# A GNN layer whose gathers are shared out: SyncE copies one more pair of tiles per 16 octets, row by row

## The chip, the core and the metric

The kernel runs on one core of a Trainium2 chip. The metric is the device time of one execution in microseconds (us); lower is better. TensorE, VectorE, ScalarE, GpSimd and SyncE appear in the profile as PE (PEld for its weight loads), DVE, ACT, POOL and SP.

## The reference

One layer of a graph network with 12500 nodes of 64 features and 400000 edges of 16 features; the edges are sorted by their target node dst, their source nodes src are random. Afterwards x gets the layer's result added and is normalised.

```python
m_in = jnp.concatenate([x[src], x[dst], edge_attr], axis=-1)
h = jax.nn.silu(m_in @ W1 + b1)
messages = jax.nn.silu(h @ W2 + b2)
agg = jax.ops.segment_sum(messages, dst, num_segments=x.shape[0])
node_in = jnp.concatenate([x, agg], axis=-1)
y = jax.nn.silu(node_in @ W3 + b3)
x = _layernorm(x + y, axis=-1)
```

W1 is 144 x 64: its first 64 rows (W1a below) act on x[src], the next 64 on x[dst], the last 16 on the edge's own features.

## The kernel before

The edges come in 3125 tiles of 128. Eight tiles make an octet (391 octets, the last with five tiles), three octets a chunk. Because dst is sorted, the targets of a chunk lie in a window of 112 nodes.

The product x W1a is made once, in the first octets, and stored in device memory as the table pa, 12500 rows of 64 floats (256 bytes). From octet 9 on (RAW) an octet needs, for each of its 1024 edges, the row of pa (or, equally, of x) that src names. There are two ways to get it.

- `gather` (L290 to L300): GpSimd issues one indirect DMA per tile, which fetches 128 rows by a column of indices into `ga`. The tile pool of `ga` has AHEAD + 2 = 5 buffers, and octet o + 3 is gathered in the loop's pass o, so a gather waits until TensorE has read the octet five before it.
- `columns` (L245 to L266): for the first two tiles of some octets (the list `pairs`, 153 octets), ScalarE and VectorE copy columns of x, which lies transposed in SBUF as `xs`, into a tile `cx`. Each copy moves 4 bytes in 64 partitions from an address in a register. ScalarE copies 2 x 24 columns per octet and VectorE 2 x 28. The registers are loaded many at a time (L261) from a row of byte offsets `cxi`, which SyncE fetches from src (`index`, L277) and VectorE scales (`address`, L285).

`first_layer` (L348) adds, on TensorE, the part of the window and of the edge's features (L357), the column pairs times W1a (L368) and the gathered rows, transposed by a product with the identity (L370, one product per two tiles). ScalarE applies silu (L374, tile `h`). `second_layer` (L377) multiplies by W2 (L383, L385), ScalarE applies silu again (L389, tile `m`), and `add_up` (L392) multiplies m by `eh`, which marks each edge's target within the window (L398). VectorE makes `oh` and `eh` by comparisons (`compare_dst`, L337; `compare_nodes`, L344).

`load` (L321) is SyncE's main work: for each octet it copies 448 KB of target indices into `dr` (L326, two buffers) and 64 KB of edge features into `oh` (L328, three buffers). Once per chunk it also loads the window's columns `xr` at an address from a register (`window_load`, L303 and L307).

Each engine executes its instructions in the order in which the loop over octets (L509) writes them; a `manual_schedule` keeps that order for TensorE, ScalarE, VectorE and SyncE. In pass o the order of the calls is: `index(o + 3)`, `gather(o + 3)`, `load(o + 2)`, `compare_dst(o + 1)`, VectorE's first columns, `first_layer(o)`, `compare_nodes(o + 1)`, VectorE's second columns, `add_up(o - 2)`, `second_layer(o - 1)`, `address(o + 2)`, and then work on the nodes that are complete (with loads `xa` and stores `out` on SyncE) at the passes given in a table `todo`.

Of the kernel before, what the change touches and what calls it, by code (L numbers as in the profile page):

```python
# [9 lines left out]
F32 = mybir.dt.float32  # L10
BF16 = mybir.dt.bfloat16
I32 = mybir.dt.int32
U8 = mybir.dt.uint8
AF = mybir.ActivationFunctionType
OP = mybir.AluOpType
# [3 lines left out]
ENG = mybir.EngineType  # L19

P = 128
# [6 lines left out]
RAW = 9  # L28
TABLES = 4
ACOLS = (24, 24)  # L30
VCOLS = (28, 28)
ALOAD = 16
XBASE = (0, 64 << 18)
XADDR = 35840
# [59 lines left out]
def windows(ctx, tc, ident, badi, pa, x, xt, src_c, src_row, dst_c, dst_row, attr_t, base, w1, b1, w2, b2, w3, b3, out, edges):  # L94
    nc = tc.nc
    N, D = x.shape
# [69 lines left out]
    def resident(s, c):  # L166
        w = min(XC, NP - c)
        nc.sync.dma_start(xs[s * D:(s + 1) * D, c:c + w], xt[:, c:c + w])
# [41 lines left out]
    for k in range(3):  # L210
        t = fast.tile([P, D], F32, name=f"xw{k}")
# [3 lines left out]
    octs = []  # L215
# [4 lines left out]
    with tc.tile_pool(name="gat", bufs=AHEAD + 2) as gat, tc.tile_pool(name="drp", bufs=2) as drp, \  # L220
# [4 lines left out]
            tc.tile_pool(name="ps2", bufs=2, space=PSUM) as ps2, \  # L225
            tc.tile_pool(name="psa", bufs=1, space=PSUM) as psa, \
            tc.tile_pool(name="cx", bufs=4) as cx, tc.tile_pool(name="cxi", bufs=3) as cxi, \
            tc.tile_pool(name="nx", bufs=2) as nx, tc.tile_pool(name="nv", bufs=1) as nv:
        got, loaded, made = {}, {}, {}


        RATE = sum(ACOLS) + sum(VCOLS)
        pairs = []
        while True:
            o = RAW + -(-2 * P * (len(pairs) + 1) // RATE) + 1
# [6 lines left out]
        def columns(o, eng, part):  # L242
# [5 lines left out]
            else:  # L248
                lo, n, copy = lo + sum(ACOLS) + sum(VCOLS[:part]), VCOLS[part], nc.vector.tensor_copy
            hi = lo + n  # L250
            while lo < hi:
                j, e0 = lo // (2 * P), lo % (2 * P)
                if j >= len(pairs):
                    return
                n = min(hi - lo, P - e0 % P, ALOAD if eng == ENG.Activation else P)
                if pairs[j] not in cols:
# [8 lines left out]
                    copy(t[h, 4 * e:4 * e + 4], xb[h, ds(r - (XBASE[s] + XADDR), 4)])  # L265
                lo += n  # L266

        def begun(o):

            first, behind = -(-(o - RAW) * RATE // (2 * P)), -(-(o + 1 - RAW) * RATE // (2 * P))  # L270
            return range(max(0, first), max(0, min(behind, len(pairs))))

        def index(o):
            for j in begun(o):
                t = cxi.tile([1, 2 * P], I32, name="cxi")
                e = octs[pairs[j]][1] * P
                nc.sync.dma_start(t, src_row[:, e:e + 2 * P])  # L277
                indices[j] = t

        def address(o):  # L280
            for j in begun(o):
                t = indices[j]
                for s in range(2):
                    h = slice(s * P, (s + 1) * P)
                    nc.vector.tensor_scalar(t[:, h], t[:, h], 4.0, float(XBASE[s] + XADDR), op0=OP.mult, op1=OP.add)  # L285
# [4 lines left out]
        def gather(o):  # L290
            c, t0, n, first, last = octs[o]
            ga = gat.tile([P, OT, D], F32, name="ga")
            sc = srcs[t0 // SCT][:, t0 % SCT:]
            if n % 2:
                nc.vector.memset(ga[:, n, :], 0.0)
            for i in range(2 if o in pairs else 0, n):
                nc.gpsimd.indirect_dma_start(  # L297
                    out=ga[:, i, :], out_offset=None, in_=x if o < RAW else pa[:, :],
                    in_offset=bass.IndirectOffsetOnAxis(ap=sc[:, i:i + 1], axis=0))
            got[o] = ga  # L300
# [32 lines left out]
        def compare_dst(o):  # L333
            c, t0, n, first, last = octs[o]
            n2 = n + n % 2
            dr, oh = loaded.pop(o)
            nc.vector.tensor_tensor(oh[0:W, :n2 * P], dr[:, :n2 * P], wn[0:W, c:c + 1].to_broadcast([W, n2 * P]),  # L337
                                    op=OP.is_equal)
            hots[o] = [oh]

        def compare_nodes(o):
            c, t0, n, first, last = octs[o]
            eh = ehp.tile([P, OT, W], F32, name="eh")
            nc.vector.tensor_tensor(eh[:, :n], winrow[c][:, None, :].to_broadcast([P, n, W]),  # L344
                                    dc[:, t0:t0 + n, None].to_broadcast([P, n, W]), op=OP.is_equal)
            hots[o].append(eh)

        def first_layer(o):  # L348
            c, t0, n, first, last = octs[o]
            n2 = n + n % 2  # L350
            k = n2 // 2
            ga = got.pop(o)
            oh, eh = hots.pop(o)
            p1 = ps1.tile([P, OT // 2, P], F32, name="p1")
            ohv = oh.rearrange("p (i s e) -> p s i e", s=2, e=P)
            for s in range(2):
                nc.tensor.matmul(p1[s * D:(s + 1) * D, :k], xw[c % 3], ohv[:, s, :k], start=True, stop=False,  # L357
                                 skip_group_check=True)
            if o < RAW:
                pt = mis.tile([P, OT // 2, P], F32, name="mm")  # L360
                for i in range(k):
                    nc.tensor.matmul(pt[:, i, :], ga[:, 2 * i:2 * i + 2, :].rearrange("p s d -> p (s d)"), ident,  # L362
                                     start=True, stop=True)
                xg = work.tile([P, OT // 2, P], F32, name="m")
                nc.vector.tensor_copy(xg[:, :k], pt[:, :k])
                nc.tensor.matmul(p1[:, :k], w1d, xg[:, :k], start=False, stop=True, skip_group_check=True)
            if o in pairs:
                nc.tensor.matmul(p1[:, 0, :], w1d, cols.pop(o), start=False, stop=False, skip_group_check=True)  # L368
            for i in range(1 if o in pairs else 0, k if o >= RAW else 0):
                nc.tensor.matmul(p1[:, i, :], ga[:, 2 * i:2 * i + 2, :].rearrange("p s d -> p (s d)"), ident,  # L370
                                 start=False, stop=(i == k - 1), skip_group_check=True)
            columns(o, ENG.Activation, 0)
            h = work.tile([P, OT // 2, P], F32, name="h")
            nc.scalar.activation(h[:, :k], p1[:, :k], AF.Silu, bias=b1s)  # L374
            made[o] = h, eh
# [106 lines left out]
        for q in range(early):  # L482
            o = lead[due[q]] + 2
# [4 lines left out]
        for q0 in range(0, rest, RB):  # L488
            o = lead[due[q0 + RB - 1]] + 2
# [16 lines left out]
        with tc.manual_schedule(engines={ENG.PE, ENG.Activation, ENG.DVE, ENG.SP}):  # L506
            compare_dst(0)
            compare_nodes(0)
            for o in range(NO + 1):  # L509
                if o == 0:  # L510
                    sources(0, slice(CT, SCT))
                    for c in range(0, NP, XC):
                        resident(0, c)
                    nc.sync.dma_start(dc[:, CT:], dst_c[:, CT:])
                    for k in range(0, NP, 2048):
                        n = min(2048, NP - k)
                        nc.scalar.activation(agg[:, k:k + n], zero.to_broadcast([P, n]), AF.Copy)
                for c in tables[o * per:(o + 1) * per]:
                    table(c)
                if o == RAW:  # L520
                    nc.vector.memset(mv, 1.0)
                    nc.vector.memset(eps, 1e-5)
                if 1 <= o < 1 + len(range(0, NP, XC)):
                    resident(1, (o - 1) * XC)
                index(o + 3)
                if o % (SCT // OT) == 6 and (o // (SCT // OT) + 1) * SCT < TILES:
                    sources(o // (SCT // OT) + 1)
                if o + AHEAD < NO:
                    gather(o + AHEAD)
                if o + 2 < NO:  # L530
                    load(o + 2)
                    if octs[o + 2][3]:
                        window_load(octs[o + 2][0])
                if o + 1 < NO:
                    compare_dst(o + 1)
                columns(o, ENG.DVE, 0)
                if o >= 3 and octs[o - 3][4]:
                    add_window(octs[o - 3][0])
                if o < NO:
                    first_layer(o)  # L540
                if o + 1 < NO:
                    if octs[o + 1][3] and o:
                        window_copy(octs[o + 1][0])
                    compare_nodes(o + 1)
                columns(o, ENG.DVE, 1)
                if o >= 2:
                    add_up(o - 2)
                if o >= 1:
                    second_layer(o - 1)
                if o + 2 < NO and octs[o + 2][3]:  # L550
                    window_product(octs[o + 2][0])
                address(o + 2)
                if o < NO:
                    for f, a in todo.get(o, []):
                        f(*a)
# [294 lines left out]
```

## Time and profile before

| | us |
|---|---|
| median of 3 timed runs | 4885.05 |
| lowest and highest of them | 4879.56, 4898.01 |
| profiled execution, its own time | 4706.3 |
| its span, first to last instruction | 4704.4 |
| busy: PE, DVE, POOL, ACT | 2870.6, 2903.5, 2695.6, 2421.6 |
| mean granted TensorE clock in it | 0.686 of full speed |

A group line of the profile gives line, engine, operation, tile written <- tile read, count | busy us, mean ns of one | idle us just before them, and what ended most of that. A line of a wait list gives engine, tile and line <- what ended the wait: us in total, times, longest. A line of one source line's view gives count: shortest/median/longest ns, first and last start. A timeline line begins with start and length in us. Register loads (TENSOR_LOAD), moves and the issue of DMAs run on an engine's sequencer (SPq, DVEq, ACTq) and are not counted as busy, so SyncE has no busy time on the page at all.

### The profile page before, as it was taken

The page shows a single profiled execution, that of the slowest core. Times are in us where ns is not written, and L with a number is a line of the kernel's source. Part 1 is how long each engine was busy: PE and PEld are TensorE (multiplying, and loading weights), DVE is VectorE, ACT ScalarE, POOL GpSimd, SP SyncE. Part 2 cuts the span into 40 slices and gives each one's busy share as a digit, 9 for nine tenths or more (in the row PEclk, how much of TensorE's full clock was granted, in tenths as well). Part 3 has the DMA queues.
Part 4 walks back from the last instruction along what each step waited for, and adds up shares of the span by engine and source line. Part 5 has one row for each costly group of instructions (what it writes and reads, how often), then busy time and mean ns, then how long its engine had stood idle before and what let it go on. Part 6 is the DMA issues. An engine that isn't in the chain of part 4 may idle for free. (4 is left out here: it accounts for less than half of the span.)

```text
span 4704.4 us, 84644 instructions
## 1 busy us (share of the span) xinstructions
PE 2870.6 (61%) x15387; PEld 1914.5 (41%) x15387; DVE 2903.5 (62%) x22948; ACT 2421.6 (51%) x18926; POOL 2695.6 (57%) x2828
## 2 busy tenths in 40 slices
PE   4756656565665666565665565656655566565666
PEld 3434434343443444343443343434433444343444
DVE  1466666666666656666666666566656666666665
ACT  1255555555555555555555555555555555555554
POOL 4655555565565655555555555555565655555553
PEclk8776676676666667676666666667666666666667
DMA  5322222222222222222222222222222222222222
GB/s 129 83 67 67 69 68 67 67 68 67 67 73 67 69 63 69 69 66 69 67 67 72 69 68 67 64 67 67 72 63 64 73 68 72 63 67 68 66 68 58
DMA packets 188666, 326.32 MB, mean 69 GB/s; under 512 B 83880, under 2 KB 92076, under 8 KB 187228
## 3 DMA queue, kind: packets, MB, share of 16 engines
q1 hardware_dynamic: 84176, 224.95, 15.1%
q0 software_dynamic: 90208, 92.55, 10.5%
q10 hardware_dynamic: 13740, 3.32, 0.3%
q14 instruction: 413, 3.38, 0.2%
q8 instruction: 129, 2.11, 0.2%
HBM read 314.18 MB, written 6.40 MB: 68 GB/s over the span
## 5 line engine op out<-in xcount | busy, mean ns | idle before, releaser
L297 POOL DMA_INDIRECT ga<-pa,sc x2747 | 2626.3, 956 | 1889.1 <-issue 702.3
L265 DVE COPY cx<-xs 64x4 uint8 x21072 | 1821.9, 196 | 1080.0 <-issue 1051.2
L265 ACT COPY cx<-xs 64x4 uint8 x18096 | 1927.4, 188 | 1025.0 <-issue 983.5
L398 PE MATMUL pg<-eh,m 128*64 128x112 f32 x6250 | 596.4, 359 | 1729.1 <-ACT m L389 766.4
L398 PEld LDWEIGHTS pg<-eh,m 128*64 128x64 f32 x6250 | 479.4, 197 | 1810.5 <-ACT m L389 837.3
L385 PE MATMUL p<-w2d,h 128*128 128x128 f32 x3126 | 710.6, 396 | 13.1 <-issue 13.0
L389 ACT ACTIVATE m<-p 128x512 f32<-128x512 f32 x391 | 232.3, 594 | 857.5 <-remote 404.2
L385 PEld LDWEIGHTS p<-w2d,h 128*128 128x128 f32 x3126 | 605.1, 287 | 163.5 <-issue 163.2
L357 PE MATMUL p<-oh,xw 128*64 128x512 f32 x1564 | 630.2, 898 | 1.1 <-issue 1.0
L337 DVE TENSOR_TENSOR oh<-dr,wrow 112x1024 f32<-112x1024 int32 x391 | 473.5, 1211 | 165.6 <-issue 160.1
L344 DVE TENSOR_TENSOR eh<-wrow,dc 128x896 f32<-128x896 f32 x391 | 424.6, 1086 | 224.4 <-issue 134.7
L370 PEld LDWEIGHTS p<-ident,ga 128*128 128x128 f32 x2748 | 423.6, 234 | 289.3 <-issue 257.2
L370 PE MATMUL p<-ident,ga 128*128 128x128 f32 x2748 | 481.8, 327 | 0.0
L374 ACT ACTIVATE h<-p,b1s 128x512 f32<-128x512 f32 x391 | 267.0, 683 | 227.9 <-ACT cx L265 58.5
L383 PE MATMUL p<-b2r,one 3*128 3x512 bf16 x391 | 210.3, 538 | 0.0
L368 PEld LDWEIGHTS p<-cx,w1d 128*128 128x128 f32 x306 | 58.6, 240 | 199.5 <-issue 199.5
L357 PEld LDWEIGHTS p<-oh,xw 128*64 128x64 f32 x1564 | 101.7, 179 | 59.7 <-issue 27.3
L297 POOL DMA_INDIRECT ga<-in_x,sc x72 | 68.1, 946 | 66.0 <-PE mm L362 39.9
L285 DVE TENSOR_SCALAR cxi<-cxi 1x128 int32<-1x128 int32 x306 | 59.2, 235 | 65.1 <-issue 62.9
L368 PE MATMUL p<-cx,w1d 128*128 128x128 f32 x306 | 93.9, 397 | 0.0
L312 PE MATMUL mm<-w1ab,xr 64*112 64x64 f32 x262 | 78.0, 396 | 7.9 <-DMA xr<-in_xt 6.8
L383 PEld LDWEIGHTS <-one 3*128 3x128 bf16 x391 | 37.6, 96 | 93.5 <-issue 77.0
(71 smaller groups left out, 710.2 us busy)
## 6 DMA issues: line engine op xcount, KB each, us to landing
dr<-in_dst_row SPq DMA_DIRECT2D x390, 448.0 KB
ga<-pa,sc POOLq DMA_INDIRECT x2747
oh<-in_attr_t SPq DMA_DIRECT2D x390, 64.0 KB
xs<-in_xt SPq DMA_DIRECT2D x12, 512.0 KB
xr<-in_xt SPq DMA_DIRECT2D x131, 28.0 KB
pa<-v ACTq DMA_DIRECT2D x24, 128.0 KB
xa<-in_x SPq DMA_DIRECT2D x24, 128.0 KB
out<-v SPq DMA_DIRECT2D x24, 128.0 KB
```

The lines of the kernel that those rows point to most:

```text
L265: copy(t[h, 4 * e:4 * e + 4], xb[h, ds(r - (XBASE[s] + XADDR), 4)])
L297: nc.gpsimd.indirect_dma_start(out=ga[:, i, :], out_offset=None, in_=x if o < RAW else pa[:, :], in_offset=bass.IndirectOffsetOnAxis(ap=sc ...
L337: nc.vector.tensor_tensor(oh[0:W, :n2 * P], dr[:, :n2 * P], wn[0:W, c:c + 1].to_broadcast([W, n2 * P]), op=OP.is_equal)
L344: nc.vector.tensor_tensor(eh[:, :n], winrow[c][:, None, :].to_broadcast([P, n, W]), dc[:, t0:t0 + n, None].to_broadcast([P, n, W]), op=OP. ...
L357: nc.tensor.matmul(p1[s * D:(s + 1) * D, :k], xw[c % 3], ohv[:, s, :k], start=True, stop=False, skip_group_check=True)
L368: nc.tensor.matmul(p1[:, 0, :], w1d, cols.pop(o), start=False, stop=False, skip_group_check=True)
L370: nc.tensor.matmul(p1[:, i, :], ga[:, 2 * i:2 * i + 2, :].rearrange("p s d -> p (s d)"), ident, start=False, stop=(i == k - 1), skip_group ...
L374: nc.scalar.activation(h[:, :k], p1[:, :k], AF.Silu, bias=b1s)
L383: nc.tensor.matmul(p2[:, :n2, :], one3, b2r[:, :n2, :], start=True, stop=False, skip_group_check=True)
L385: nc.tensor.matmul(p2[:, 2 * i:2 * i + 2, :].rearrange("p s d -> p (s d)"), h[:, i, :], w2d, start=False, stop=(i == k - 1), skip_group_ch ...
L389: nc.scalar.activation(m[:, :n2], p2[:, :n2], AF.Silu)
L398: nc.tensor.matmul(pg[s * D:(s + 1) * D, :], m[:, i, :], eh[:, i, :], start=(first and i < 2), stop=(last and i >= n - 2), skip_group_chec ...
```

## The change

From octet 9 on, a second list of octets, `rpairs` (one in 16), has its tiles 2 and 3 (its second pair) not gathered. In each pass `rows(o)` has SyncE load 16 byte offsets into registers and issue 16 DMAs, each of one 256-byte row of pa, from device memory to one partition of a tile `rx`; after 16 octets the pair's 256 rows are there, and `first_layer` multiplies `rx` in place of `ga`. The offsets come from src as for the columns: SyncE fetches 256 indices (`rload`, in front of the loads of a pass), and VectorE multiplies them by the 256 bytes of a row (`raddress`, behind `address`). `rows(o)` stands behind the loads of pass o and in front of its node work.

```diff
+ROWS = 16
...
+            tc.tile_pool(name="rx", bufs=2) as rx, tc.tile_pool(name="rxi", bufs=2) as rxi, \
...
+        rpairs = []
+        while True:
+            o = RAW + -(-2 * P * (len(rpairs) + 1) // ROWS) + 1
+            if o >= len(octs) - 1:
+                break
+            rpairs.append(o)
+        single, rindex = {}, {}
+        pab = pa[:, :].bitcast(U8).rearrange("n d -> (n d)")
+
+        def rows(o):
+            lo = (o - RAW) * ROWS
+            j, e0 = lo // (2 * P), lo % (2 * P)
+            if o < RAW or j >= len(rpairs):
+                return
+            if e0 == 0:
+                single[rpairs[j]] = rx.tile([P, 2, D], F32, name="rx")
+            t = single[rpairs[j]].bitcast(U8)
+            _, regs = nc.values_load_multi_w_load_instructions(
+                rindex[j][0:1, e0:e0 + ROWS], engines=(ENG.SP,), min_val=0, max_val=4 * D * (N - 1),
+                skip_runtime_bounds_check_because="src names a node")
+            for e, r in zip(range(e0, e0 + ROWS), regs):
+                nc.sync.dma_start(t[e % P:e % P + 1, e // P, :], pab[ds(r, 4 * D)].rearrange("(o n) -> o n", o=1))
+
+        def rbegun(o):
+            j = (o - RAW) * ROWS // (2 * P)
+            return o >= RAW and (o - RAW) * ROWS % (2 * P) == 0 and j < len(rpairs), j
+
+        def rload(o):
+            yes, j = rbegun(o)
+            if yes:
+                rindex[j] = rxi.tile([1, 2 * P], I32, name="rxi")
+                e = (octs[rpairs[j]][1] + 2) * P
+                nc.sync.dma_start(rindex[j], src_row[:, e:e + 2 * P])
+
+        def raddress(o):
+            yes, j = rbegun(o)
+            if yes:
+                nc.vector.tensor_scalar(rindex[j], rindex[j], 4.0 * D, None, op0=OP.mult)
...
-            for i in range(2 if o in pairs else 0, n):
+            for i in range(n):
+                if o in (pairs, rpairs)[i // 2 % 2] and i < 4:
+                    continue
                 nc.gpsimd.indirect_dma_start(
...
-                nc.tensor.matmul(p1[:, i, :], ga[:, 2 * i:2 * i + 2, :].rearrange("p s d -> p (s d)"), ident,
+                g2 = single.pop(o) if o in rpairs and i == 1 else ga[:, 2 * i:2 * i + 2, :]
+                nc.tensor.matmul(p1[:, i, :], g2.rearrange("p s d -> p (s d)"), ident,
                                  start=False, stop=(i == k - 1), skip_group_check=True)
...
                 index(o + 3)
+                rload(o + 3)
...
                 address(o + 2)
+                raddress(o + 2)
+                rows(o)
```

## The prediction

> **What bounds the kernel now.** I read the page first, for the share of each engine and the costliest groups, then the list of waits, then a stretch of the timeline, then the single lines that show SyncE's own instructions (the page counts none of them as busy).
>
> ```profile
> PE 2870.6 (61%) x15387; PEld 1914.5 (41%) x15387; DVE 2903.5 (62%) x22948; ACT 2421.6 (51%) x18926; POOL 2695.6 (57%) x2828
> ...
> L297 POOL DMA_INDIRECT ga<-pa,sc x2747 | 2626.3, 956 | 1889.1 <-issue 702.3
> L265 DVE COPY cx<-xs 64x4 uint8 x21072 | 1821.9, 196 | 1080.0 <-issue 1051.2
> L265 ACT COPY cx<-xs 64x4 uint8 x18096 | 1927.4, 188 | 1025.0 <-issue 983.5
> ```
>
> No engine is full by its busy time. A gather takes POOL 944 ns and a gap of 0.30, so 1.245 us from one to the next, and an octet has 7.2 of them on average (2819 over 391). With the 2 us before an octet's first gather POOL needs about 11 us. An octet lasts 11.78 us: the first and last matmul of L370 start at 189.0 and 4678.9 us and 381 octets lie between them. So POOL looks nearly full, and the question is who waits for whom.
>
> ```profile
> PEld pg L398 <- ACT m L389: 837.3, 189, 8.8
> POOL ga L297 <- PE p L370: 654.9, 135, 16.4
> PEld p L370 <- DMA ga<-pa,sc: 32.1, 23, 1.6
> SPq L326 <- DVE oh L337: 2043.5, 245, 14.1
> ```
>
> POOL waits 655 us for TensorE to read a buffer; TensorE waits 32 us for a gather in the whole kernel. The gathers run ahead, as far as five buffers let them:
>
> ```profile
> 2017.63 2.08 PE L370 MATMUL p<-ident,ga 128*128 128x128 f32 x8
> 2019.98 0.94 POOL L297 DMA_INDIRECT ga<-pa,sc  x1 [2.23 <-PE p L370]
> ```
>
> The gather at 2019.98 starts 0.27 us after those matmuls end, because it takes their buffer. It is for the octet five later. TensorE has more than three octets of rows in store, so gathers don't set the pace. VectorE and ScalarE do: each copies its columns in order, loses about 1000 us to "issue" between copies (the trace does not say why), and TensorE waits for their eh and m. SyncE idles: its load of dr waits 2043 us for VectorE's comparison to free one of two buffers.
>
> **The change part by part.** First, the pairs. rpairs starts at octet 26 and takes every 16th up to 378, so 23 pairs, 46 gathers. POOL is relieved of 46 x 1.245 = 57 us. Its cover is the store above: POOL merely waits longer for buffers. Worth 0 here; -57 if POOL set the pace. TensorE multiplies the same tiles; the only new thing there is waits for SyncE's transfers, landed more than an octet earlier: 0.
>
> Second, VectorE: 23 times one tensor_scalar over 1x256. The same over 1x128 (L285) takes 208 ns median. Between 0.21 and twice 0.235, I take 0.35: 8 us, counted in full since VectorE is on the path. Behind it in VectorE's queue stands the next comparison, which SyncE's load waits for. Its own wait, for the 1 KB of indices that SyncE asked for an iteration before, should be over; if not, it costs some us, 23 times.
>
> Third, SyncE. Its own instructions, one view per line:
>
> ```profile
> L261 DVEq TENSOR_LOAD <-cxi x893: 342/1848/2124, 183.6 to 4645.4; - x179
> ...
> L303 DVEq TENSOR_LOAD <-bi x131: 302/309/564, 3.9 to 4655.8; - x131
> L303 SPq TENSOR_LOAD <-bi x131: 270/468/658, 4.7 to 4658.5; - x131
> ...
> L277 SPq DMA_DIRECT2D cxi<-in_src_row x153: 14/259/873, 137.0 to 4567.5; - x153
> ...
> L307 SPq MOVE xr<-in_xt x131: 19/38/690, 5.5 to 4658.9; - x131
> L307 SPq DMA_DIRECT2D xr<-in_xt x131: 13/491/728, 5.6 to 4659.0; - x131
> ...
> L168 SPq DMA_DIRECT2D xs<-in_xt x14: 465/472/811, 11.5 to 148.1; - x14
> ```
>
> Each octet from 9 to 376 gets one load of 16 registers and 16 row transfers: 368 loads, 5888 transfers of 256 B. The register load: VectorE takes 309 ns for one register and 1848 for its usual 28, so 57 ns for each further one; SyncE's 468 + 15 x 57 gives 1.32 us. Here a rule speaks against the change: the Trainium skill (Runtime: NRT & Kernel Launch, Instruction fetch mechanics) puts such loads at about 200 ns a register "even for bulk"; that would be 3.2 us. The rows say 57, and I use them, but keep 3.2 as an end.
>
> One row transfer exists nowhere in the trace: one run, one partition, address from a register. Its nearest rows: the index load (one run, one partition, fixed address) 259 ns; the window load xr (64 partitions, register address) 491. The table xs, 64 partitions at a fixed address, takes 472, so the register adds about 20 ns. So 0.28, and I take 0.30. Around it a MOVE of 38 ns and two gaps of about 0.05 (of that size between L303, the MOVE and L307's transfer): 0.44 us a row. Ends: 0.40, and 0.72 with xr's 491, the 41 ns ALU_OP it needs and a further gap. The 16 rows are 7.0 us (6.4 to 11.5).
>
> SyncE's present work in an octet: dr 0.317 + oh 0.374 + a third of xr's chain (0.468 + 0.041 + 0.038 + 0.491) 0.35 + 0.39 index loads 0.10 + gaps 0.25 = 1.4 us. With the change 1.4 + 1.3 + 7.0 = 9.7 of 11.78 us; by the skill's figure 11.6, full to the brim. SyncE decides above (11.78 - 1.4 - 1.3) / 16 = 0.57 us a row.
>
> What SyncE is late with: behind the rows stand the next octet's dr and oh, and an xa or out at times. dr is issued when a comparison ends (2011.10) and is needed two comparisons later, about 21 us on. From its issue to its landing dr takes 2.9 us (median in the trace). That cover of 18 us takes the 8.3 us of loads and rows, as long as SyncE keeps up on average. If the cover were gone, every us of SyncE would count: 8.3 x 368 = 3050 us, the worst bound.
>
> The transfers themselves: page row q1 has 84176 packets for 15.1% of 16 engines' span, 0.135 us each. The skill (DMA: Bandwidth & Descriptors, Why a DMA increments its semaphore by 16 and not by 1) says that a one-partition transfer runs on one DMA engine, the lowest-numbered. No view here shows it; as an estimate, 16 rows and 16 semaphore writes at 0.135 are 4.3 us an octet on that engine, beside the 3.1 us of its 26% share. It delays loads by 4 us at most, inside the 18. Spread over 16 engines it is 0.3. I take 0.
>
> Sum: 0 + 8 + 0 = +8 us on the profiled execution, 4706.3 (span 4704.4 and 1.9 around it). The three timed runs have a median of 4885.05, 1.038 times as much; the trace cannot say why, and I carry the sum over by that ratio: 4714 x 1.038 = 4893.
>
> **The rivals.** *SyncE becomes the bound* (slower). It has the dearest price per row in the change, a gather costs POOL 1.245 / 128 = 10 ns a row against 440 here. For it: 9.7 of 11.78 us leaves little, and 0.57 a row is inside my ends. Against it: xs beside xr. At 0.60 a row SyncE needs 12.3 us an octet, 0.5 x 368 = 190 us more: 4896, or 5080 timed; at 0.72, 14.2 us and +900: about 5800. If each row also waited for the one before it to land in the same tile, it would be far worse than that; the diff shows disjoint partitions, so I give that little.
>
> *Small losses on VectorE and ScalarE* (slower). SyncE's late index and xa loads stall VectorE now and then, or the 16 register transfers lengthen the "issue" gaps. 2 us on each of 16 to 30 occasions and the 8 us: +40 to +70 profiled, about 4940.
>
> *The gathers did count* (faster). In the timed runs, which are longer than the profiled one, POOL might be later than here. For it: 11 of 11.78 us. Against it: 655 us of waiting the other way. Then -57 + 8: 4657, or 4834 timed.
>
> *The change does nothing that it says*: rows fetched too late would show as TensorE waiting at L370; they are asked for one octet ahead or more, so it is the same as no gain.
>
> **How the numbers follow.** A measurement of this kernel can tell about 0.5%, 24 us, from no change. No effect beyond that: 0.47. SyncE as bound: 0.28. Small losses: 0.12. Gathers count: 0.13. So faster 0.13, same 0.47, slower 0.40. The likeliest alone spans 4870 to 4909. The range goes from 4850, which takes in half a gain, to 5090, which takes in the small losses and SyncE just over its limit (a row at 0.60); dearer rows and the full gain are left out, some 2 in 10.
>
> **What would show it.** Right: POOL's wait for PE p L370 grows by about 57 us, PE still waits under 50 us for gathers, SyncE's row transfers take near 0.30 us and its load 1.3, the SPq wait for DVE oh shrinks from 2043 us by most of 368 x 8.3 without VectorE waiting for dr. Wrong: "DVE oh <- DMA dr" grows from 2.8 us to hundreds, or row transfers near 0.5 us with no wait left at L326 (SyncE is the bound); DVE's issue gaps grow by over 100 us (a cost I don't have); or POOL's wait falls while the span gets shorter (gathers counted).

## The result, and the profile after

The change made the kernel slower: 5140.73 us median against 4891.53 in the runs beside it, a ratio of 1.0508 (95% interval 1.0467 to 1.0549). The prediction said 4893, no change, with a range from 4850 to 5090. The profiled execution took 5136.94 us.

The page after, first its busy times, then the three groups that answer to those of before (line numbers have moved by 2 to 45):

```profile
PE 2890.8 (56%) x15387; PEld 1933.6 (38%) x15387; DVE 2941.7 (57%) x22971; ACT 2422.1 (47%) x18926; POOL 2639.9 (51%) x2782
...
L341 POOL DMA_INDIRECT ga<-pa,sc x2701 | 2570.6, 952 | 2367.2 <-PE p L415 1217.2
L267 DVE COPY cx<-xs 64x4 uint8 x21072 | 1849.0, 193 | 1314.6 <-issue 1263.3
L267 ACT COPY cx<-xs 64x4 uint8 x18096 | 1919.5, 188 | 1040.3 <-issue 1006.8
```

The work is the same (46 gathers fewer, 23 instructions of VectorE more) in a span 431 us longer. Not all of that is the change's: the timed runs differ by 249 us, and the profile of before, at 4706 us, was 185 us faster than the runs of before beside the change. VectorE loses 1263 us to "issue" between copies instead of 1051, and GpSimd waits 1217 us for TensorE instead of 655 (1181 to 1197 and 1100 to 1126 in three repeats of the changed kernel, below). So GpSimd is even further ahead, and everybody else is later. TensorE's own work has grown by 20 us only, at a granted clock of 0.660 instead of 0.686.

The list of waits after (waiting engine, tile and line <- what ended the wait: us, times, longest):

```profile
PEld mm L356 <- DMA xr<-in_xt: 519.6, 73, 13.5
...
DVE oh L381 <- DMA dr<-in_dst_row: 49.4, 28, 3.4
...
SPq L370 <- DVE oh L381: 68.7, 16, 15.5
```

SyncE waited 2043 us for VectorE before; 69 are left. The loads `dr` still come in time: VectorE waits 49 us for them. New is TensorE's wait of 520 us (142 to 316 in the repeats) for `xr`, the window's columns, which SyncE loads and TensorE needs in the same pass.

What the new instructions cost, from the views of single lines (count: shortest/median/longest ns):

```profile
L292 SPq MOVE rx<-pa x5888: 3/29/1434, 192.4 to 4976.7; - x197
L292 SPq DMA_DIRECT2D rx<-pa x5888: 3/228/1437, 192.4 to 4976.7; - x197
...
L288 SPq TENSOR_LOAD <-rxi x368: 4/980/1216, 191.1 to 4971.4; - x184
```

The medians are below my estimates. The longest are not: a MOVE of 29 ns can take 1434. The timelines of SyncE, GpSimd and VectorE (start, length, line, tile, count) show when:

```profile
2007.50 5.11 SPq L292 DMA_DIRECT2D rx<-pa  x16
2014.83 9.40 SPq L292 DMA_DIRECT2D rx<-pa  x16
```

```profile
2012.82 0.94 POOL L341 DMA_INDIRECT ga<-pa,sc  x1 [9.89 <-PE p L415]
...
2019.06 0.94 POOL L341 DMA_INDIRECT ga<-pa,sc  x1 [0.30 <-issue]
2024.89 1.12 POOL L341 DMA_INDIRECT ga<-pa,sc  x1 [4.89 <-PE p L415]
```

```profile
2020.75 0.17 DVE L267 COPY cx<-xs 64x4 uint8 x1 [0.51 <-issue]
2021.45 1.89 DVE L267 COPY cx<-xs 64x4 uint8 x23 [0.54 <-issue]
```

The first sixteen rows fall into GpSimd's pause from 2003 to 2013 and take 0.32 us each. The next sixteen run beside a burst of gathers. From 2015.8 to 2021.4 four rows advance in steps of about 0.71 us, two of them to a row (one for the MOVE, one for the transfer): 1.44 us a row. VectorE's copies take steps of the same length there (2020.75 to 2021.45). I call it a step when a copy starts 0.62 to 0.80 us after the copy just before it on its engine; most follow at 0.1 or less. The trace of before has 1535 steps, 744 on ScalarE and 791 on VectorE, and all but 12 lie between 4 us after the first gather of a burst (gathers less than 1 us apart) and 2 us after the end of its last, which is 57% of the span. (The expectations below counted by other limits.) The trace of after has 1717. I had read them as "issue", of unknown cause, and left them aside. In the mean of after, 16 rows take 9.1 us from the first transfer's start to the last one's end, 0.59 a row.

### The profile page after: what moved, and what is told of

Its sections match the earlier page's. It is cut to its first block, busy times and chain, and to the rows that moved or that the text cites. A ratio compares the mean times of both kernels' runs of the same rounds, so it can differ in the third digit from the quotient of the medians.

```text
span 5135.2 us, 96948 instructions
## 1 busy us (share of the span) xinstructions
PE 2890.8 (56%) x15387; PEld 1933.6 (38%) x15387; DVE 2941.7 (57%) x22971; ACT 2422.1 (47%) x18926; POOL 2639.9 (51%) x2782
## 5 line engine op out<-in xcount | busy, mean ns | idle before, releaser
L341 POOL DMA_INDIRECT ga<-pa,sc x2701 | 2570.6, 952 | 2367.2 <-PE p L415 1217.2
L267 DVE COPY cx<-xs 64x4 uint8 x21072 | 1849.0, 193 | 1314.6 <-issue 1263.3
L430 PE MATMUL p<-w2d,h 128*128 128x128 f32 x3126 | 681.5, 386 | 3.0 <-issue 2.3
L430 PEld LDWEIGHTS p<-w2d,h 128*128 128x128 f32 x3126 | 582.6, 279 | 145.6 <-issue 145.6
L415 PEld LDWEIGHTS p<-ident,ga 128*128 128x128 f32 x2702 | 455.2, 252 | 296.7 <-issue 275.5
L415 PE MATMUL p<-ident,ga 128*128 128x128 f32 x2702 | 518.0, 347 | 0.0
L356 PEld LDWEIGHTS mm<-w1ab,xr 64*112 64x112 f32 x262 | 56.1, 271 | 614.2 <-DMA xr<-in_xt 519.6
```

The source lines that it names most:

```text
L341: nc.gpsimd.indirect_dma_start(out=ga[:, i, :], out_offset=None, in_=x if o < RAW else pa[:, :], in_offset=bass.IndirectOffsetOnAxis(ap=sc ...
L415: nc.tensor.matmul(p1[:, i, :], g2.rearrange("p s d -> p (s d)"), ident, start=False, stop=(i == k - 1), skip_group_check=True)
L430: nc.tensor.matmul(p2[:, 2 * i:2 * i + 2, :].rearrange("p s d -> p (s d)"), h[:, i, :], w2d, start=False, stop=(i == k - 1), skip_group_ch ...
```

## The experiments

The runs took place on three chips, which are not alike: before took 4694 to 4724 us on two of them (A and B here, both with steps of 0.71 us) and 3612 on the third (C, without). On which chip the first comparison ran is not on record; the forecasts of e1 and e5 in us were made for its before of 4892 us, and are read here as shares of that. Every ratio is to before on the same chip.

**Is it the late window?** e1_window_early, chip A:

```diff
-                    if octs[o + 2][3]:
-                        window_load(octs[o + 2][0])
+                if o + 3 < NO and octs[o + 3][3]:
+                    window_load(octs[o + 3][0])
```

> The changed kernel, but SyncE loads a chunk's window xr one pass earlier (in pass o for octet o + 3), so that TensorE needs it a pass later than it is issued; the 16 rows per octet stay. Theory A (the late window is the loss): the 520 us that TensorE waits for xr go, and the time falls to 4880 to 4940. Theory B (SyncE is full: about 12.4 us of work in each octet, whatever stands in front): the wait moves from xr to dr or the comparison, and the time stays above 5050. Theory C (the row transfers disturb the other engines by themselves): above 5100, and VectorE's issue gaps stay near 1260 us.

Measured: 5002.86 us, 1.0663 (1.0642 to 1.0684). The changed kernel itself was run again on both chips (r_after, c_after, d_after, below) and gave 1.058 to 1.061. The wait for xr is gone and nothing is won. TensorE waits longer for VectorE's xw instead (463 us in c_after, the changed kernel on the same chip):

```profile
PE pg L443 <- DVE xw L360: 563.3, 48, 16.5
```

So the late window was a symptom; the repeats say the same, with waits for xr of 142 to 316 us at nearly one ratio. Theory A is out; B and C both stand.

**Do the gathers make the steps?** e2_before_no_gather and e3_after_no_gather, chip A, the same edit on the kernel before and the changed one:

```diff
+        still = fast.tile([P, OT, D], F32, name="still")
+        nc.gpsimd.memset(still, 0.25)
         def gather(o):
             c, t0, n, first, last = octs[o]
+            if o >= RAW:
+                got[o] = still
+                return
```

> The kernel before, with the gathers from octet 9 on left out (TensorE multiplies a constant tile in their place). Theory D (the steps of about 0.71 us between instructions of ScalarE and VectorE come from GpSimd's gathers in flight): such steps vanish (1455 of them in the profile of before), the issue gaps at L265 fall from about 1000 us on each engine to under 400, and the time to 3900 to 4400. Rival E (the steps come from something else, such as the 512 KB loads per octet or TensorE's clock): they stay within 30% of their number, and the time stays at 4600 to 4890.

> The changed kernel with the gathers from octet 9 on left out (a constant tile in their place); SyncE's rows stay and are multiplied. Theory D: every row costs SyncE about 0.32 us, 16 of them 5.1 us instead of a mean of 9.1, TensorE's wait for xr is under 60 us, and the time is that of the kernel before without gathers within 1.5%. Rival E: 16 rows still take about 9 us in the mean, and the time is 3% or more above the kernel before without gathers.

Measured: 3105.42 us without gathers on the kernel before, 0.662 of it (0.660 to 0.663), and 3293.91 us on the changed one, 0.702 (0.7005 to 0.703). Of the steps 12 and 14 are left. Groups of before without gathers, and the rows' line of the changed kernel without them:

```profile
L265 ACT COPY cx<-xs 64x4 uint8 x18096 | 1787.4, 189 | 101.1 <-issue 66.9 <-DVE oh L343 11.0 <-DVE v L451 5.2
L265 DVE COPY cx<-xs 64x4 uint8 x21072 | 1614.0, 180 | 227.3 <-issue 195.5 <-DVE oh L343 8.6 <-ACT cx L265 3.5
```

```profile
L292 SPq MOVE rx<-pa x5888: 29/29/38, 173.6 to 3181.5; - x197
L292 SPq DMA_DIRECT2D rx<-pa x5888: 227/228/317, 173.6 to 3181.6; - x197
```

The issue gaps fall from 984 and 1051 us to 67 and 196, and no row takes longer than 0.36 us. Theory D holds: the steps come with the gathers. The gain is far larger than the 3900 to 4400 us expected for e2, which also spares GpSimd's work and the gathers' traffic. That e3 is 6% above e2 and waits 640 us for xr misses its expectations (within 1.5%, under 60 us), for another reason: its octet lasts 8.1 us (from the matmuls, as in the prediction), and SyncE has about 7.7 to do (an estimate: 1.4 as before, 1.0 for the register load, 5.3 for the rows). There SyncE is full without any steps.

**What is GpSimd's relief worth?** e5_relief_only, chip A: the 46 gathers left out, a constant tile in their place, no rows.

```diff
+        still = fast.tile([P, 2, D], F32, name="still")
+        nc.gpsimd.memset(still, 0.25)
...
             if e0 == 0:
-                single[rpairs[j]] = rx.tile([P, 2, D], F32, name="rx")
+                single[rpairs[j]] = still
+            return
...
-                rload(o + 3)
...
-                raddress(o + 2)
```

> The kernel before with only the 46 gathers of the second pairs left out: TensorE multiplies a constant tile there, SyncE copies no rows and VectorE scales no offsets. The prediction's step (POOL is ahead, its relief is worth nothing): 4870 to 4905, no difference from before. Rival (POOL set the pace in the timed runs): 57 us less, 4820 to 4845.

Measured: 4645.66 us, 0.9907 (0.988 to 0.9934), between the two expectations. TensorE waits 33 us for gathers, no less than before, since there is nothing to save; but by the ratio 46 gathers fewer are 44 us (31 to 56), 0.95 each. A likely reason is that bursts end sooner and with them the steps of the others (1415 are left of 1535); no run tests it.

**Is SyncE full, or do the rows disturb?** Four kernels on chip B, r_after being the changed kernel itself.

> The changed kernel again, beside the next three on one chip (the chips differ: before took 4892 us on one and 4694 on another). All theories: 1.045 to 1.06 of before.

r_after: 5001.68 us, 1.0584 (1.0543 to 1.0626).

```diff
# e4_fixed_rows
-            _, regs = nc.values_load_multi_w_load_instructions(
-                rindex[j][0:1, e0:e0 + ROWS], engines=(ENG.SP,), ...
...
-            for e, r in zip(range(e0, e0 + ROWS), regs):
-                nc.sync.dma_start(t[e % P:e % P + 1, e // P, :], pab[ds(r, 4 * D)].rearrange("(o n) -> o n", o=1))
+            for e in range(e0, e0 + ROWS):
+                r = 4 * D * ((lo + e * 47) % N)
+                nc.sync.dma_start(t[e % P:e % P + 1, e // P, :], pab[r:r + 4 * D].rearrange("(o n) -> o n", o=1))
# e6_rows_only
-                if o in (pairs, rpairs)[i // 2 % 2] and i < 4:
+                if o in pairs and i < 2:
...
-                g2 = single.pop(o) if o in rpairs and i == 1 else ga[:, 2 * i:2 * i + 2, :]
+                g2 = ga[:, 2 * i:2 * i + 2, :]
# e7_rows8
-ROWS = 16
+ROWS = 8
```

> The changed kernel with the same 5888 row transfers, but from fixed addresses: no register load and no MOVE on SyncE, so one instruction per row instead of two (the rows fetched are not those that src names). Theory B (SyncE's instructions are the cost: with the gathers in flight each one takes a step of 0.71 us, so a row costs 1.4 us there and 0.71 with one instruction): 16 rows take 4.5 to 6.5 us instead of 9.1, SyncE waits for VectorE again by over 800 us, and the time is within 1.5% of before, 0.985 to 1.01. Theory C (the row transfers themselves disturb): above 1.03 of before.

> The changed kernel with all its rows, but the second pairs are gathered as before and the rows are read by nobody. If the relief of 46 gathers was worth the 0.9% that leaving them out alone gave, this is 0.7 to 1.2% slower than the changed kernel: 1.055 to 1.07 of before. If with SyncE full the relief is worth nothing, it equals the changed kernel within 0.3%.

> The changed kernel with 8 rows per octet instead of 16 (a pair per 32 octets: 11 pairs, 22 gathers less). Theory B: SyncE has 4.5 us of rows instead of 9.1 and so some 4 us to spare in each octet; the time is 0.99 to 1.003 of before. Theory C or a cost in proportion to the rows: half of the loss, about 1.02 to 1.03 of before.

Measured: e4_fixed_rows 4918.05 us, 1.0412 (1.0372 to 1.0451); e6_rows_only 5051.82, 1.0704 (1.0665 to 1.0744), 1.1% above r_after as the relief would have it; e7_rows8 4878.79, 1.0346 (1.0301 to 1.0392). The waits of SyncE in e7 and in e4:

```profile
SPq L370 <- DVE oh L381: 873.9, 250, 14.4
```

```profile
SPq L368 <- DVE oh L379: 759.2, 252, 14.9
```

e4's rows take 7.0 us, where 4.5 to 6.5 were expected. In both SyncE stands waiting for VectorE again, and TensorE waits under 8 us for xr, so SyncE is neither full nor late where it was; the loss is still 3.5 and 4.1%. Theory B alone falls. For e7 theory C had 1.02 to 1.03: half the rows cost more than half of the loss. ScalarE and VectorE take 744 and 791 steps in the profile of before; in e7 it is 915 and 851, in r_after 902 and 870. The rows slow the others beside them, by something other than SyncE being late.

**The instructions or the bytes?** e8_one_transfer (later c_one_transfer) fetches 16 neighbouring rows by one DMA at a fixed address; e9_semaphores_only (later c_semaphores_only) puts 32 instructions per octet on SyncE of the kernel before, which only increment a semaphore:

```diff
# one transfer
-            _, regs = nc.values_load_multi_w_load_instructions(
...
-            for e, r in zip(range(e0, e0 + ROWS), regs):
-                nc.sync.dma_start(t[e % P:e % P + 1, e // P, :], pab[ds(r, 4 * D)].rearrange("(o n) -> o n", o=1))
+            r = 4 * D * ((lo + e0 * 47) % (N - ROWS))
+            e = e0 % P
+            nc.sync.dma_start(t[e:e + ROWS, e0 // P, :], pab[r:r + 4 * D * ROWS].rearrange("(o n) -> o n", n=4 * D))
# semaphores only; a load whose value nobody uses leaves its semaphore increment
+        def idle_steps(o):
+            if RAW <= o <= 376:
+                for k in range(32):
+                    nc.values_load(bi[0:1, k:k + 1], engines=(ENG.SP,), min_val=0, max_val=N - 1, ...)
...
                 address(o + 2)
+                idle_steps(o)
```

The first try fell on chip C:

> The changed kernel with the 16 rows of an octet fetched by one DMA (16 neighbouring rows of pa at a fixed address, not those that src names): the same bytes, one instruction instead of 33 on SyncE. If SyncE's instructions are the cost: 0.985 to 0.997 of before, that is the 0.9% of relief or part of it. If the transfers or the offsets' handling (rload, raddress, the tile rx) are the cost: 1.02 to 1.05.

> The kernel before with 32 more instructions per octet on SyncE where the rows would stand (octets 9 to 376, 11776 in all), none of which moves data: each only increments a semaphore that nobody waits on for it. If any instruction on SyncE disturbs the other sequencers while gathers are in flight: 1.03 to 1.08 of before, ScalarE's and VectorE's steps of 0.71 us up by 100 or more each. If it takes DMAs to disturb: 0.995 to 1.01, and the steps stay near 960 and 900.

Measured on C: 3554.71 us, 0.9858 (0.9838 to 0.9879), and 3611.78 us, 1.0003 (0.9995 to 1.0011). On this chip e9 shows 11 steps in the whole trace, and GpSimd does set the pace. TensorE waits for the gathers:

```profile
PE p L377 <- DMA ga<-pa,sc: 751.4, 478, 6.3
```

There 46 gathers fewer are worth 57 us (3611.73 - 3554.71), what the prediction's rival had for them, and instructions on SyncE cost nothing: 32 of them take it 1.95 us. For the question this was no answer, so both ran again, on chip A, beside the changed kernel:

> The changed kernel beside the next two. The chips fall in two kinds: on those where SyncE, ScalarE and VectorE take steps of 0.71 us while gathers are in flight, before takes 4690 to 4890 us; on one without such steps it took 3612 us and TensorE waited for gathers. On a chip with steps: 1.045 to 1.06 of before again. On one without: SyncE's rows cost 0.32 us each, it has 8 of 9.2 us to do and is late at times; if the relief of GpSimd (46 x 1.245 = 57 us) prevails, 0.985 to 0.995 of before; if the late window loads prevail, 1.00 to 1.02.

> One DMA of 16 neighbouring rows per octet in place of 16 DMAs (fixed addresses). On a chip with steps: 0.985 to 0.997 of before if SyncE's instructions are the cost of the change, 1.02 to 1.05 if the rows' bytes or the handling of the offsets are. On a chip without steps: 0.986 again.

> 32 more instructions per octet on SyncE that move no data. On a chip with steps: 1.03 to 1.08 of before if any instruction on SyncE disturbs the other sequencers, 0.995 to 1.01 if it takes DMAs. On a chip without steps: 1.000 again.

Measured: c_after 4990.67 us, 1.0606 (1.0573 to 1.0639); c_one_transfer 4695.44, 0.9984 (0.9968 to 1.0000); c_semaphores_only 4952.29, 1.0527 (1.0495 to 1.0559). The new instructions' line and four waits of c_semaphores_only, then two of c_one_transfer:

```profile
L273 SPq EVENT_SEMAPHORE  x11776: 1/17/1404, 187.8 to 4808.3; - x200
```

```profile
DVE cx L265 <- issue: 1173.7, 1773, 4.4
ACT cx L265 <- issue: 1158.7, 1729, 6.2
...
PE mm L319 <- DMA xr<-in_xt: 7.3, 2, 3.8
...
SPq L333 <- DVE oh L344: 600.0, 237, 15.9
```

```profile
DVE cx L267 <- issue: 1024.0, 1589, 4.1
ACT cx L267 <- issue: 1006.9, 1706, 3.9
```

This settles what costs the time. The rows' bytes, the offsets' load and scaling, the tile rx and the 368 transfers left cost some 0.8% together: c_one_transfer gains 0.16% (just short of its forecast of 0.3% or more) where e5 gained 0.9%, and its trace has 1543 steps, before 1535. 11776 instructions with a median of 17 ns, which move nothing and which nobody waits for, cost 249 us. They lengthen the issue gaps of ScalarE by 175 us and of VectorE by 123 against the profile of before, and the steps are 1773. SyncE isn't late there: TensorE waits 7 us for xr, VectorE 1 for dr, and SyncE itself 600 for VectorE. But it is not idle either: beside the gathers an octet's 32 take 8.6 us in the mean instead of 1.95.

The 5.3% are three quarters of the 7.0% that the rows cost without the relief (e6, chip B). The cost does not go by the number of instructions alone: e4's 5888 transfers cost about 5% (4.1 and the relief's 0.9), nearly as much.

**If the sequencers compete, fewer copies must help.** e10_fewer_columns and e11_still_fewer leave the rows out and shorten the lists of columns:

```diff
-ACOLS = (24, 24)
-VCOLS = (28, 28)
+ACOLS = (20, 20)     # e11: (16, 16)
+VCOLS = (24, 24)     # e11: (20, 20)
```

> The kernel before with 2 x 20 and 2 x 24 columns per octet instead of 2 x 24 and 2 x 28 (more gathers, fewer copies), no rows on SyncE. From the relief run a gather costs about 0.95 us of the whole; 16 copies less save ScalarE 0.76 and VectorE 0.57 us per octet. If those two set the pace: 0.965 to 0.99 of before. If gathers cost more than that or GpSimd becomes the bound: 1.00 to 1.02.

> As the one before, with 2 x 16 and 2 x 20 columns. If ScalarE and VectorE still set the pace: 0.94 to 0.97 of before. If GpSimd's 11.5 us per octet become the bound: no better than with 2 x 20 and 2 x 24, 0.97 to 1.0, and TensorE begins to wait for gathers.

On chip C: 3665.44 us, 1.0161 (1.0143 to 1.018), and 3728.63, 1.033 (1.0312 to 1.0348), the second beyond both its forecasts. GpSimd is the bound there, and each of the 46 and 94 gathers more costs 1.17 to 1.24 us. Again on a chip with steps, B:

> The changed kernel once more, for the chip that this call gets. With steps of 0.71 us: 1.05 to 1.065 of before. Without them (before near 3612 us): 0.985 to 0.995 if GpSimd's relief prevails, 1.00 to 1.02 if SyncE's late window loads do.

> 2 x 20 and 2 x 24 columns per octet instead of 2 x 24 and 2 x 28, no rows on SyncE. On a chip with steps, if every instruction of ScalarE, VectorE and SyncE competes there, 16 copies less per octet (6100 in all) give back what 6100 instructions on SyncE cost, some 2.5%, and 47 more gathers take 1%: 0.975 to 0.995 of before. If GpSimd's gathers weigh more: 1.00 to 1.015. On a chip without steps: 1.016 again.

> 2 x 16 and 2 x 20 columns. On a chip with steps: 0.95 to 0.985 of before if the instructions weigh most, 1.00 to 1.03 if GpSimd becomes the bound. On a chip without steps: 1.033 again.

Measured: d_after 4980.21 us, 1.0591 (1.0552 to 1.0631); d_fewer_columns 4476.26, 0.9536 (0.9498 to 0.9574); d_still_fewer 4445.16, 0.9464 (0.9429 to 0.95). The copies of d_fewer_columns:

```profile
L265 DVE COPY cx<-xs 64x4 uint8 x18144 | 1620.1, 194 | 1097.6 <-issue 1072.7
L265 ACT COPY cx<-xs 64x4 uint8 x15136 | 1638.1, 188 | 1029.0 <-issue 983.9
```

The first step down gained 4.6% where 0.5 to 2.5 were expected. But it doesn't show that the sequencers compete. The copies themselves take 289 us less on ScalarE and 202 less on VectorE than in the profile of before, and the issue gaps are what they were there (983.5 and 1051.2). So the 227 us gained can be the copies' own time, on two engines that set the pace. Only d_still_fewer has shorter gaps (436 and 882 us), and it gains 31 us more. The version that beats both kernels on a chip with steps has fewer copies and more gathers; on a chip without steps it is 1.6 to 3.3% slower than before. The changed kernel itself was not measured on chip C.

## Why the prediction was wrong

*The price at nothing.* The step that failed is the third one of the change: SyncE's work was costed against SyncE's own spare time alone, at 0. The 11776 MOVEs and row transfers have a cost for ScalarE and VectorE, which wait for nothing of theirs. It stood among the rivals, in the small losses on VectorE and ScalarE, at 40 to 70 us; as many instructions without any data cost 249 in c_semaphores_only. The prediction's own sign of a missing cost came: VectorE's issue gaps grew by over 100 us (130 to 212 in the changed kernel's four profiles).

*The row's price.* 0.44 us estimated; 0.34 in the mean without gathers (e3), 1.44 in a step stretch, 0.59 in the mean of after. The derivation from xs, xr and the index load was right for the instruction alone; what it lacked is the stretching beside a burst. This term was 7.0 us an octet and measured 9.1. The register load was 1.32 and measured 0.98, VectorE's scaling 0.35 and measured 0.27.

*What SyncE is late with.* The prediction named dr, oh, xa and out, and 18 us of cover. It left out xr, issued and needed in the same pass, with hardly any cover: 142 to 520 us of TensorE's waits. But e1 showed that it isn't the cause.

*SyncE as the bound.* The rival's number came near: at 0.60 a row 5080, and 0.59 and 5141 were measured. SyncE was indeed full in the changed kernel, as that rival's own sign said: rows over 0.5 us and hardly a wait left for dr's buffer (69 us). As a cause it carries part at most, so the nearness is partly luck: with SyncE waiting again, e7 and e4 still lose 3.5 and 4.1%. How much of the last 2% is SyncE's lateness and how much its longer instructions, the runs do not separate.

*The relief.* Costed at 0 because the gathers run ahead. That reading of the waits was right on the chips with steps (TensorE waits 21 us for gathers in after too), and the conclusion wrong: e5 gives 44 us for 46 gathers. On chip C, where the gathers do set the pace, it is 57.

*The transfers themselves.* Taken at 0. No run tests this alone, as c_one_transfer spreads its rows over DMA engines (16 semaphore writes to a transfer), but the packets leave little. The section of the Trainium skill that was named for one DMA engine to a row (DMA: Bandwidth & Descriptors, Why a DMA increments its semaphore by 16 and not by 1) goes by the access pattern's shape, and says that software can split a contiguous run over more engines. The trace of after agrees with one: on SyncE's queue it has 5888 more packets of 256 bytes, one to a row, and 5911 more of 4 bytes, a semaphore write for each row and each of the 23 index loads. Packets of these sizes took 15 and 10 ns in the mean, so 16 rows are 0.4 us and not 4.3; the 135 ns were the mean of a queue mostly of 4 KB packets.

*The skill's 200 ns a register* (the Trainium skill, Runtime: NRT & Kernel Launch, Instruction fetch mechanics) would have had SyncE full, by a term that is not so: 16 registers took 0.98 us, 61 each.

*The ratio of 1.038* between the timed runs and the profiled execution has a likely reason in the chips: before took 4694, 4704, 4724 and 3612 us on those of the experiments. After's own profiled and timed runs agree within 0.1%.

## What to carry to other kernels

An engine that idles is not free to use: before giving a sequencer thousands of small instructions, look whether others show issue gaps of one fixed length, and count instructions on every engine that has them, not only busy time. An issue gap that the trace doesn't explain is a term of its own; here such gaps were about 1000 of 4704 us on each of two engines, and 221 and 247 on a chip without steps. To test a cost, take the data out and leave the instructions, then the reverse: two runs settled what five others had not.

## What was not expected of the hardware

- While bursts of indirect DMAs run on GpSimd, SyncE, ScalarE and VectorE go on in steps of about 0.71 us, often one instruction to a step. All but 12 of 1535 lie between 4 us after a burst's first gather and 2 us after its last. Without gathers the kernel takes 0.662 of its time, and 12 steps are left. What the step is, the runs do not show. It doesn't go with the loading of instructions: a packet of the instruction queue q14 is in flight from 2 us before to 1 us after the copy at 22% of the steps of before, and at 27% of moments taken at random.
- Chips differ in this: before took 4703 us on one and 3612 on another, where a trace of the nearly same kernel has 11 steps.
- In those stretches instructions on SyncE slow ScalarE and VectorE. 11776 added ones cost 249 us of the whole in c_semaphores_only, 21 ns each, and nothing on the chip without steps. They are slowed themselves: 17 ns in the median, 128 in the mean.
- A row of 256 bytes at a register's address takes SyncE 0.32 us back to back; GpSimd's gather takes 1.245 for 128 of them.
